# A guard at the start of a kernel becomes part of a decision at its end

## The chip, the cores and the metric

The kernel runs on one core of a Trainium2 chip. The metric is the time of one execution on the device, in microseconds (us); the median of several runs is given. The profile is a record of one execution by the hardware profiler. Its engines are PE (TensorE, matmuls), PEld (its weight loads), DVE (VectorE), ACT (ScalarE), POOL (GpSimd) and SP (SyncE, which here only issues DMAs). A name with q, such as SPq, is that engine's queue of DMA issues, branches and semaphore instructions.

## The reference, cut to what matters

Two layers are applied to 16 graphs of 1024 nodes with 256 features each. Layer 0 is a masked self-attention with a gelu MLP, layer 1 a graph attention; each has a residual.

```python
# layer 0
h = relu(layernorm(x))
qkv = layer_norm(h, gamma1, beta1)            # 8 heads of 32, the same for q, k and v
scores = einsum('bhqd,bhkd->bhqk', qkv, qkv) / sqrt(32)
attn = softmax(where(adj > 0, scores, -inf))
h = h + attn @ qkv
x = x + h + gelu(layer_norm(h, gamma2, beta2) @ W1 + b1) @ W2 + b2
# layer 1
f = relu(layernorm(x));  g = f @ W
logits = (g @ a_1).T + g @ a_2 + (g @ a_12) @ g.T
p = softmax(where(adj > 0, leaky_relu(logits, 0.2), -9e15))
x = x + elu(f @ W_1 + (p @ f) @ W_2)
```

## The kernel before

There are two programs for the same function. `fast_path` leaves out the running maxima of the softmaxes; that is exact enough only while the scores stay small. `general_path` computes them. The top function, `tile_gnn_kernel`, chooses.

Before the fast path it loads gamma1 and beta1 (1 KB each) into one partition (L1525), takes the largest absolute value of each on DVE (L1529), forms 16 max|gamma| + sqrt(32) max|beta| (L1533, L1534) and compares it with a constant (L1535). The result, `bounded`, is read into a register of all five engines (L1539), and each of them branches (L1540). `redo`, one minus that flag, is written at L1538. If the bound holds, `fast_path` runs. It ends with a second test: sums of squares of three weight products and a count of softmax denominators in a good interval were gathered in `seen` along the way; a matmul adds them over the partitions (L1489), four small DVE instructions turn them into `redo` (L1491 to L1496), all engines read `redo` (L1542) and branch (L1543): normally over the general path, to the end.

The fast path handles one graph ("batch", b) after another, with the work of neighbouring batches interleaved. Within it, generators ("streams") issue the instructions: `stream_a` the layer-0 attention, one step per key tile of 128, 32 steps a batch; `stream_b` the rest of layer 0 and all of layer 1 for the batch before; others load, normalize and convert masks. Each stream yields a *place*, a number in batches (1.28 is 28% into the second batch's attention); a loop (L1477 to L1482) always resumes the stream with the lowest place. So places fix the order of instructions on each engine; at the end of `fast_path` a loop (L1498 to L1507) chains all instructions of the current block to that order, engine by engine. `clock` is the planner's own estimate of elapsed time; it decides when deferred pieces are due.

The lines that matter below:

- `prologue` for batch 0: SP loads x (L770) and the mask (L831); DVE takes statistics (L725, L726), ACT rectifies (L787), DVE and POOL make the value tiles (L734, L800, L801), PE transposes them (L808).
- `g1` and `be1`, gamma1 and beta1 broadcast to 128 partitions, are loaded on ACT's queue (L636).
- In the steady part PE makes scores (L975), DVE adds the mask (L996), ACT takes the exponential (L999), PE weighs the values (L1012), and POOL's queue sums the weights by accumulating DMAs (L1036); PE's matmuls of the other layers go through the helper at L570, `po` (L1185) among them.
- `stream_s` (L1469): setup of weight products, then `check_products` from place 1.28 on, one piece per 0.04: `sq`, the square of `wm` (L710), its sum (L712), and the two small products with their sum (L714 to L716). All are DVE instructions.

Of the kernel before, what the change touches and what calls it, by code (L numbers as in the profile page):

```python
# [9 lines left out]
F32 = mybir.dt.float32  # L10
BF16 = mybir.dt.bfloat16
FP8 = mybir.dt.float8e5
I32 = mybir.dt.int32
AF = mybir.ActivationFunctionType
ALU = mybir.AluOpType
# [10 lines left out]
DEN_MIN = 1.0e-24  # L26
DEN_MAX = 1.0e36
ALPHA = 0.2


@with_exitstack
def general_path(
# [125 lines left out]
    with tc.For_i(0, B, 1) as bi:  # L158
# [262 lines left out]
        def logits(t):  # L421
            lp = sc_tile(f"lg_{b}_{t}")
            for dc in range(DC):
# [16 lines left out]

            nc.vector.scalar_tensor_tensor(e, e, ALPHA, e, op0=ALU.mult, op1=ALU.max)
            nc.vector.scalar_tensor_tensor(
                m1[:, 1:2], m1[:, 0:1], ALPHA, m1[:, 0:1], op0=ALU.mult, op1=ALU.max
            )
# [49 lines left out]
def fast_path(  # L494
# [28 lines left out]
    nc = tc.nc  # L523
    B, N, D = x.shape
# [15 lines left out]
    pool = lambda name, bufs, **kw: ctx.enter_context(tc.tile_pool(name=name, bufs=bufs, **kw))  # L540
    const = pool("const", 1)
# [11 lines left out]
    smallp = pool("smallp", 3)  # L553
# [62 lines left out]
    def broadcast_row(src, name):  # L616
        t = const.tile([P, D], F32, name=name)
        rows_to_load.append((t, bass.AP(tensor=src.tensor, offset=src.offset, ap=[[0, P], [1, D]])))
        return t
# [13 lines left out]
    g1 = broadcast_row(gamma1, "g1")  # L633
    be1 = broadcast_row(beta1, "be1")
# [28 lines left out]
    def setup():  # L663
        wl, wa, wT, wb = (lp1.tile([P, DC, D], F32, tag="e1", name=f"stage_{i}") for i in range(4))
        weights_to_load[:0] = [(wl, W), (wa, a_12)]
        for t, src in rows_to_load:
            nc.sync.dma_start(t, src)
        for t, src in weights_to_load:
            nc.sync.dma_start(t, src.rearrange("(c p) n -> p c n", p=P))
        yield  # L670

        for oc in range(DC):
            pt = ps_tile([P, DC, P], f"p_wT_{oc}")
            for ic in range(DC):
                nc.tensor.transpose(pt[:, ic, :], wl[:, ic, oc * P : (oc + 1) * P], ident)
            nc.scalar.copy(wT[:, oc, :], pt.rearrange("p c q -> p (c q)"))
        clock[0] += 0.5
        yield

        def product(dst, lhs, rhs, n, name):  # L680

            for oc in range(DC):
                pp = ps_tile([P, n], f"p_{name}_{oc}")
                for kc in range(DC):
                    matmul(
                        pp,
                        lhs[:, kc, oc * P : (oc + 1) * P],
                        rhs[:, kc, :n],
                        start=(kc == 0),
                        stop=(kc == DC - 1),  # L690
                    )
                nc.scalar.copy(dst[:, oc, :], pp)

        product(wb, wa, wT, D, "wb")
        clock[0] += 1.7
        yield
        product(wm, wT, wb, D, "wm")
        product(w_a2.unsqueeze(2), wT, a2c.unsqueeze(2), 1, "w_a2")
        product(wo2[:, :, D : D + 1], wT, a1c.unsqueeze(2), 1, "w_a1")
        nc.gpsimd.memset(wo2[:, :, D + 1 : D + 2], 0.0)  # L700
        clock[0] += 2.0
        yield

    def check_products():


        sq = lp1.tile([P, DC * D], F32, tag="e1", name="sq")
        few = smallp.tile([P, 2 * DC], F32, tag="few", bufs=1, name="few")
        wmf = wm.rearrange("p c n -> p (c n)")
        nc.vector.tensor_tensor(sq, wmf, wmf, op=ALU.mult)  # L710
        yield
        nc.vector.tensor_reduce(seen[:, 0:1], sq, axis=mybir.AxisListType.X, op=ALU.add)  # L712
        yield
        nc.vector.tensor_tensor(few[:, :DC], w_a2, w_a2, op=ALU.mult)  # L714
        nc.vector.tensor_tensor(few[:, DC:], wo2[:, :, D], wo2[:, :, D], op=ALU.mult)
        nc.vector.tensor_reduce(seen[:, 1:2], few, axis=mybir.AxisListType.X, op=ALU.add)  # L716
        yield
# [25 lines left out]
    def defer(us, f):  # L743
        deferred.append((clock[0] + us, len(deferred), f))

        return clock[0] + us
# [352 lines left out]
    def rest(b, st, tails):  # L1099
# [151 lines left out]
        def weights(c, i):  # L1251
# [18 lines left out]

            nc.vector.scalar_tensor_tensor(e, e, ALPHA, e, op0=ALU.mult, op1=ALU.max)  # L1271
            ready = defer(2.5, lambda: nc.scalar.activation(e, e, AF.Exp, bias=shift))  # L1272
# [196 lines left out]
    def stream_s():  # L1469
        yield -0.3  # L1470
        for i, _ in enumerate(setup()):
            yield 0.25 + 0.05 * i
        yield 1.28
        for i, _ in enumerate(check_products()):
            yield 1.32 + 0.04 * i

    streams = [stream_s(), stream_a(), stream_b(), stream_p(), stream_c(), stream_m()]  # L1477
    places = [next(s, None) for s in streams]
    while any(p is not None for p in places):
        i = min((p, i) for i, p in enumerate(places) if p is not None)[1]  # L1480
# [9 lines left out]
    fit = smallp.tile([1, 2], F32, tag="fit", name="fit")  # L1490
# [2 lines left out]
    nc.vector.scalar_tensor_tensor(  # L1493
        fit[:, 0:1], fit[:, 1:2], float(P * B * NT), fit[:, 0:1], op0=ALU.is_ge, op1=ALU.mult
    )
    nc.vector.tensor_scalar(redo, fit[:, 0:1], -1.0, 1.0, op0=ALU.mult, op1=ALU.add)  # L1496

    last = {}  # L1498
    for i in nc.cur_bb.bb.instructions:
# [10 lines left out]

BOUND = 72.0


def kernel(tc, x, adj, gamma1, beta1, *rest):
    nc = tc.nc
    D = x.shape[2]
    with tc.tile_pool(name="flags", bufs=1) as flags:
        flag = flags.tile([1, 1], I32, name="bounded")  # L1520
        redo = flags.tile([1, 1], I32, name="redo")
        with tc.tile_pool(name="bound", bufs=1) as pool:
            r = pool.tile([1, 2, D], F32, name="bound_rows")
            for i, src in enumerate((gamma1, beta1)):
                nc.sync.dma_start(  # L1525
                    r[:, i, :], bass.AP(tensor=src.tensor, offset=src.offset, ap=[[0, 1], [1, D]])
                )
            m = pool.tile([1, 2], F32, name="bound_max")
            nc.vector.tensor_reduce(  # L1529
                m, r, axis=mybir.AxisListType.X, op=ALU.max, apply_absolute_value=True  # L1530
            )
            s = pool.tile([1, 1], F32, name="bound_sum")
            nc.vector.tensor_scalar_mul(s, m[:, 1:2], math.sqrt(32.0))  # L1533
            nc.vector.scalar_tensor_tensor(s, m[:, 0:1], 16.0, s, op0=ALU.mult, op1=ALU.add)  # L1534
            nc.vector.tensor_scalar(  # L1535
                flag, s, math.sqrt(BOUND * math.sqrt(32.0)), None, op0=ALU.is_le
            )
        nc.vector.tensor_scalar(redo, flag, -1.0, 1.0, op0=ALU.mult, op1=ALU.add)  # L1538
        bounded = nc.values_load(flag[0:1, 0:1], min_val=0, max_val=1)  # L1539
        with tc.If(bounded > 0):  # L1540
            fast_path(tc, x, adj, gamma1, beta1, *rest, redo)
        again = nc.values_load(redo[0:1, 0:1], min_val=0, max_val=1)  # L1542
        with tc.If(again > 0):  # L1543
            general_path(tc, x, adj, gamma1, beta1, *rest)
# [28 lines left out]
```

## Time and profile before

| what | us |
|---|---|
| median of 3 runs | 3482.66 |
| lowest, highest | 3480.26, 3485.44 |
| profiled execution: span, first to last instruction | 3468.1 |
| median less that span: what lies around it | 14.5 |
| PE busy in the span | 3420.8 |
| DVE, ACT, POOL busy | 2746.2, 1858.1, 1419.9 |
| first DMA issue of the branch's rows | 0.76 |
| first load of x | 4.35 |
| first scores on PE (their mask part) | 24.33 |
| last DVE instruction, `redo` | 3462.26 |

The profiled execution is known by its span; the 14.5 us are the difference to the median of the runs. Times in the timeline count from the first instruction. An idle time in brackets is followed by an arrow to what ended it. The accumulating DMAs hold 71.4% of the time of the 16 DMA engines.

### The profile page before, as it was taken

To read this page: it belongs to the slowest core of one execution; us is meant where nothing else is said; L and a number is where in the kernel's file an instruction comes from. 1 tells how busy PE (TensorE), PEld (TensorE's weight loads), DVE (VectorE), ACT (ScalarE), POOL (GpSimd) and SP (SyncE) were. 2 spreads that over 40 slices of the span, in tenths; PEclk is the share of its full clock that TensorE was granted. 3 is DMA by queue.
4 is the path that set the end of the run, shared out by engine and by line. 5 is a ranking of instruction groups with operands and counts; after the bars stand their busy time and mean duration, and the time that the engine had idled before them with its cause. 6 is when DMAs were issued, how large, how long until landed. Compare 5 with 4: busy or idle time off the path is not lost. (4 is left out here: it accounts for less than half of the span.)

```text
span 3468.1 us, 119040 instructions
## 1 busy us (share of the span) xinstructions
PE 3420.8 (99%) x52478; PEld 1650.4 (48%) x52478; DVE 2746.2 (79%) x5194; ACT 1858.1 (54%) x2184; POOL 1419.9 (41%) x1708
## 2 busy tenths in 40 slices
PE   6899999999999999999999999999999999999998
PEld 2244444444444444444444444444444444444477
DVE  6788788787887978878887887878878778887754
ACT  5555555555555555555555555555555555555522
POOL 4444443434434344443444434344344443434220
PEclk9999999999999999999999999999999999999999
DMA  8798989899899998989999899998999989899730
GB/s 194 147 187 172 185 162 192 180 188 191 163 187 175 189 190 165 186 169 190 193 166 189 166 189 185 180 188 168 190 177 194 188 162 184 171 193 185 147 64 14
DMA packets 281906, 598.56 MB, mean 173 GB/s; under 512 B 94882, under 2 KB 130084, under 8 KB 281380
## 3 DMA queue, kind: packets, MB, share of 16 engines
q0 software_dynamic: 124416, 453.04, 71.4%
q1 hardware_dynamic: 156676, 137.56, 15.5%
q8 instruction: 414, 6.78, 0.8%
q14 instruction: 112, 0.92, 0.1%
q10 hardware_dynamic: 288, 0.26, 0.0%
HBM read 104.21 MB, written 16.78 MB: 35 GB/s over the span
## 5 line engine op out<-in xcount | busy, mean ns | idle before, releaser
L999 ACT ACTIVATE e<-e 128x1024 f32<-128x1024 f32 x852 | 895.9, 1057 | 945.9 <-DVE e L996 704.4
L1036 POOL DMA_DIRECT2D acc<-e x864 | 759.6, 896 | 1443.4 <-DMA acc<-e 636.5
L996 DVE TENSOR_TENSOR e<-s,mk 128x1024 f32<-128x1024 f32 x852 | 1004.0, 1218 | 188.3 <-PE s L975 149.4
L975 PE MATMUL s<-kT 32*64 32x512 f32 x8192 | 579.2, 615 | 2.9 <-DVE odd L996 2.2
L1012 PE MATMUL o<-e,va 128*32 128x512 f32 x3456 | 462.3, 605 | 2.1 <-ACT e L999 2.1
L570 PE MATMUL pa<-gw,e 128*32 128x258 f32 x7648 | 453.8, 380 | 0.0
L570 PE MATMUL lg<-fT,uT 128*32 128x256 f32 x7680 | 448.6, 379 | 0.0
L570 PE MATMUL ph<-yT,w 128*32 128x256 f32 x7808 | 447.7, 379 | 0.0
L570 PE MATMUL po<-w,hid 128*32 128x256 f32 x7680 | 439.7, 379 | 0.0
L570 PEld LDWEIGHTS ph<-yT,w 128*32 128x32 f32 x7808 | 259.9, 110 | 197.5 <-issue 42.1
L570 PEld LDWEIGHTS po<-w,hid 128*32 128x32 f32 x7680 | 250.9, 110 | 208.4 <-issue 61.7
L570 PEld LDWEIGHTS lg<-fT,uT 128*32 128x32 f32 x7680 | 258.9, 110 | 189.7 <-issue 38.7
L570 PEld LDWEIGHTS pa<-gw,e 128*32 128x32 f32 x7648 | 251.6, 110 | 199.5 <-issue 48.3
L1272 ACT ACTIVATE e<-e,shift 128x512 f32<-128x512 f32 x256 | 183.2, 717 | 187.1 <-DVE e L1271 159.8
L1266 DVE SCALAR_TENSOR_TENSOR e<-lg,gw,mk 128x256 f32<-128x256 f32 x512 | 223.2, 477 | 71.6 <-PE lg L570 61.1
L1169 DVE TENSOR_TENSOR hid<-ph,b1c 128x512 f32<-128x512 f32 x256 | 175.4, 688 | 86.3 <-PE ph L570 74.8
L1012 PEld LDWEIGHTS o<-e,va 128*32 128x32 f32 x3456 | 69.0, 108 | 353.3 <-issue 221.5
L1271 DVE SCALAR_TENSOR_TENSOR e<-e 128x512 f32<-128x512 f32 x256 | 195.4, 763 | 8.8
L999 ACT ACTIVATE acc<-acc 128x1024 f32<-128x1024 f32 x124 | 131.0, 1057 | 130.4 <-DVE acc L996 125.9
L975 PEld LDWEIGHTS s<-kT 32*64 32x64 f32 x8192 | 121.2, 130 | 163.0 <-issue 106.2
L996 DVE TENSOR_TENSOR acc<-s,mk 128x1024 f32<-128x1024 f32 x124 | 146.1, 1218 | 20.9 <-PE s L975 18.4
L800 POOL TENSOR_TENSOR nrm<-nrm,g 128x256 f32<-128x256 f32 x128 | 114.0, 891 | 61.4 <-DVE nrm L734 61.4
(146 smaller groups left out, 3815.6 us busy)
## 6 DMA issues: line engine op xcount, KB each, us to landing
acc<-e POOLq DMA_DIRECT2D x864, 512.0 KB, 6.1
adj<-in_adj_dram SPq DMA_DIRECT2D x248, 256.0 KB, 5.3
h<-in_x_dram SPq DMA_DIRECT2D x64, 256.0 KB, 5.9
xb<-in_x_dram SPq DMA_DIRECT2D x128, 128.0 KB, 5.1
out_dram<-z SPq DMA_DIRECT2D x128, 128.0 KB, 3.7
adj<-in_adj_dram SPq DMA_DIRECT2D x4, 512.0 KB, 6.6
mk<-mq SPq DMA_TRANSPOSE x128, 6.4
w<-in_L_gnn_W_dram SPq DMA_DIRECT2D x2, 1024.0 KB
```

The source lines that it names most:

```text
L570: nc.tensor.matmul(out[c : c + HD], lhsT[:, c : c + HD], rhs, start=start, stop=stop)
L800: nc.gpsimd.tensor_mul(nrm, nrm, g1)
L975: nc.tensor.matmul(sc[j // 2][c : c + P // 2, j % 2, :], kT[r, g, kt * P + c : kt * P + c + P // 2], kT[r, g, qs], start=j >= by_pe, stop= ...
L996: nc.vector.tensor_tensor(e, masked, mb, op=ALU.add)
L999: weights = lambda e=e, masked=masked: nc.scalar.activation(e, masked, AF.Exp, scale=SCALE)
L1012: nc.tensor.matmul(o[j * HD : (j + 1) * HD, :], va[:, kt, (g * GH + j) * HD : (g * GH + j + 1) * HD], es[j // 2][:, j % 2, :], start=(kt = ...
L1036: nc.gpsimd.dma_start(sums[g, qh][i], e, accum_op=ALU.add)
L1169: nc.vector.tensor_tensor(hid[:, f0 : f0 + 2, :], ph, b1c[:, f0 : f0 + 2].unsqueeze(2).to_broadcast([P, 2, CW]), op=ALU.add,)
L1266: nc.vector.scalar_tensor_tensor(e[:, j, :], lg[:, j, :], gw[:, kt, D : D + 1], st[c // 2][:, kt // 2, qs, kt % 2], op0=ALU.add, op1=ALU.add,)
L1271: nc.vector.scalar_tensor_tensor(e, e, ALPHA, e, op0=ALU.mult, op1=ALU.max)
L1272: ready = defer(2.5, lambda: nc.scalar.activation(e, e, AF.Exp, bias=shift))
```

## The change

The top function now calls `fast_path` at once, with no loads, no flag, no register and no branch ahead of it. The bound is worked out inside `check_products`, as a new first piece, from one partition of `g1` and `be1`, which are in SBUF anyway. The result, `not_bounded`, is 0 or -1 in a constant tile; the last DVE instruction takes it as a factor: redo = fit x not_bounded + 1, where the factor was the constant -1. The pieces of `check_products` are now four, 0.03 of a batch apart, where there were three, 0.04 apart; `sq` moves to 1.32, its sum to 1.35, the small products to 1.38. If the bound does not hold, the fast path has run for nothing and the general path follows; before, the fast path was skipped.

```diff
+    not_bounded = const.tile([1, 1], F32, name="not_bounded")
+
     def check_products():
 
+        m = smallp.tile([1, 2], F32, tag="bound", bufs=1, name="bound_max")
+        for i, r in enumerate((g1, be1)):
+            nc.vector.tensor_reduce(
+                m[:, i : i + 1], r[0:1], axis=mybir.AxisListType.X, op=ALU.max, apply_absolute_value=True
+            )
+        s = smallp.tile([1, 1], F32, tag="bound_sum", bufs=1, name="bound_sum")
+        nc.vector.tensor_scalar_mul(s, m[:, 1:2], math.sqrt(32.0))
+        nc.vector.scalar_tensor_tensor(s, m[:, 0:1], 16.0, s, op0=ALU.mult, op1=ALU.add)
+        nc.vector.tensor_scalar(
+            not_bounded, s, math.sqrt(BOUND * math.sqrt(32.0)), -1.0, op0=ALU.is_le, op1=ALU.mult
+        )
+        yield
 
         sq = lp1.tile([P, DC * D], F32, tag="e1", name="sq")
...
         for i, _ in enumerate(check_products()):
-            yield 1.32 + 0.04 * i
+            yield 1.32 + 0.03 * i
...
-    nc.vector.tensor_scalar(redo, fit[:, 0:1], -1.0, 1.0, op0=ALU.mult, op1=ALU.add)
+    nc.vector.tensor_scalar(redo, fit[:, 0:1], not_bounded, 1.0, op0=ALU.mult, op1=ALU.add)
...
     with tc.tile_pool(name="flags", bufs=1) as flags:
-        flag = flags.tile([1, 1], I32, name="bounded")
         redo = flags.tile([1, 1], I32, name="redo")
-        with tc.tile_pool(name="bound", bufs=1) as pool:
-            r = pool.tile([1, 2, D], F32, name="bound_rows")
-            for i, src in enumerate((gamma1, beta1)):
-                nc.sync.dma_start(
-                    r[:, i, :], bass.AP(tensor=src.tensor, offset=src.offset, ap=[[0, 1], [1, D]])
-                )
-            m = pool.tile([1, 2], F32, name="bound_max")
-            nc.vector.tensor_reduce(
-                m, r, axis=mybir.AxisListType.X, op=ALU.max, apply_absolute_value=True
-            )
-            s = pool.tile([1, 1], F32, name="bound_sum")
-            nc.vector.tensor_scalar_mul(s, m[:, 1:2], math.sqrt(32.0))
-            nc.vector.scalar_tensor_tensor(s, m[:, 0:1], 16.0, s, op0=ALU.mult, op1=ALU.add)
-            nc.vector.tensor_scalar(
-                flag, s, math.sqrt(BOUND * math.sqrt(32.0)), None, op0=ALU.is_le
-            )
-        nc.vector.tensor_scalar(redo, flag, -1.0, 1.0, op0=ALU.mult, op1=ALU.add)
-        bounded = nc.values_load(flag[0:1, 0:1], min_val=0, max_val=1)
-        with tc.If(bounded > 0):
-            fast_path(tc, x, adj, gamma1, beta1, *rest, redo)
+        fast_path(tc, x, adj, gamma1, beta1, *rest, redo)
         again = nc.values_load(redo[0:1, 0:1], min_val=0, max_val=1)
```

More of the change, by code (lines that the diff above doesn't have):

```diff
@@ L28 @@
 ALPHA = 0.2
+BOUND = 72.0
 @with_exitstack
@@ L1507, in fast_path @@
         last[i.engine] = i.name
-BOUND = 72.0
 def kernel(tc, x, adj, gamma1, beta1, *rest):
```

## The prediction

> **What bounds the kernel now.** I read the page's first two parts, then a table of stages (busy time of each engine per stretch), then the timeline of the first 30 us and of 198 to 234 us, where the new work lands, and last the records of the two branch lines.
>
> ```profile
> span 3468.1 us, 119040 instructions
> ...
> PE 3420.8 (99%) x52478; PEld 1650.4 (48%) x52478; DVE 2746.2 (79%) x5194; ACT 1858.1 (54%) x2184; POOL 1419.9 (41%) x1708
> ```
>
> TensorE (PE) is busy for 99% of the span: all but 47 us. The page's slices show where those are, at the two ends above all, and the table of stages says it in numbers (columns: stretch, its length, busy time of PE, PEld, DVE, ACT, POOL with instruction counts, granted clock, DMA share, GB/s):
>
> ```profile
> 0.00:4.35 4.35, 0.00 (x0) 0.00 (x0) 1.25 (x5) 0.00 (x0) 0.21 (x4) 1.00 0.00 0
> 4.35:24.30 19.95, 2.65 (x8) 1.37 (x8) 13.18 (x43) 4.26 (x7) 11.46 (x21) 1.00 0.71 203
> ...
> 31.60:200.00 168.40, 155.07 (x2032) 53.97 (x2024) 129.60 (x205) 99.54 (x112) 75.33 (x90) 0.98 0.81 168
> 200.00:3380.00 3180.00, 3177.97 (x50046) 1528.05 (x50039) 2555.70 (x4823) 1723.63 (x2015) 1330.73 (x1591) 1.00 0.91 177
> ```
>
> In the first 4.35 us PE does nothing and no input of the real work is under way. From 200 to 3380 us PE waits 2.0 us of 3180. What happens in the first 4.35 us is in the timeline (start, duration, engine, line, operation):
>
> ```profile
> 0.76 0.35 SPq L1525 DMA_DIRECT2D bound_rows<-in_L_gnn_gamma_dram  x1
> 1.16 0.22 SPq L1525 DMA_DIRECT2D bound_rows<-in_L_gnn_beta_dram  x1
> 2.49 0.67 DVE L1529 TENSOR_REDUCE bound_max<-bound_rows 1x2 f32<-1x512 f32 x1 [2.49 <-DMA bound_rows<-in_L_gnn_beta_dram]
> ...
> 3.73 0.14 DVE L1538 TENSOR_SCALAR redo<-bounded 1x1 int32<-1x1 int32 x1
> 4.35 0.36 SPq L770 DMA_DIRECT2D h<-in_x_dram  x1
> 4.47 1.28 ACT L611 ACT_TABLE_LOAD   x1 [4.47 <-DVE redo L1538]
> ```
>
> Everything the kernel needs starts behind this chain: SP's first load of x at 4.35, ACT's table load at 4.47, POOL's identity at 4.49.
>
> **The change part by part.** *The start, removed.* SP's first DMA issue is at 0.76. With the two 1 KB loads, the five DVE instructions (2.49 to 3.87), the register load (465 ns on SP) and the compare-and-branch (44 ns) gone, that first issue is the load of x, and it moves from 4.35 to 0.76: **-3.59 us**. Does all else move by as much? ACT and POOL wait for nothing else, so theirs move by about 3.8 to 4.0 and get slack. The next chain begins with x's landing: DVE's first statistics at 7.05, rectify 11.50, value 15.89, transpose 18.66, first scores at 24.33. Each was released by the one before it, back to SP's loads; gamma's and beta's broadcast (ACT queue, 7.04 and 9.36) wait for the landings of the first two SP loads, by their semaphores, and move along. So the whole front moves by 3.59, and since PE has no slack after 200 us, the end does too.
>
> *The five instructions, moved and re-shaped.* They come back at place 1.28 of the schedule, where `sq` (L710) stands now, on DVE at 205.84. One 1x512 reduce took 0.674; it becomes two of 1x256. The rows around are 0.285 for 126 columns (L1097) and 0.679 for 512 (L712), a slope of 1.02 ns per column, so I take 0.42 each. The three small ones took 0.50 from 3.20 to 3.70. Sum 1.38 us of DVE. `sq` (0.68) moves one step on, to where its reduce was (0.68), the reduce goes one further, the three small ones (0.43) last. So DVE gains 0.70 net at 205.8, nothing at 217.3, at most 0.68 near 221 and 0.43 near 227. No DMA is added: the rows g1 and be1 are in SBUF since the start.
>
> What is behind them in DVE's queue, and who waits:
>
> ```profile
> 205.84 0.68 DVE L710 TENSOR_TENSOR sq<-wm 128x512 f32<-128x512 f32 x1
> ...
> 207.28 5.36 PE L570 MATMUL po<-w,hid 128*32 128x256 f32 x96
> ...
> 207.35 2.34 DVE L996 TENSOR_TENSOR e<-s,mk 128x1024 f32<-128x1024 f32 x2
> ...
> 208.59 2.19 ACT L999 ACTIVATE e<-e 128x1024 f32<-128x1024 f32 x2 [0.19 <-DVE e L996]
> ```
>
> The masked scores end at 209.69 and the exponentials at 210.78. PE's next scores (which overwrite the banks) load at 212.57 and its weighted sums at 213.62, both behind its own 5.36 us of `po`; so 2.84 us of cover lie there. Near 221 it is the same: exponentials end at 223.58, wanted at 226.35, 2.77 us. I take the cost as **0**. Without cover it is 1.38; below zero nothing can come of it, since an instruction is added. The shorter steps of the schedule (0.03 for 0.04) change nothing else: the planner's clock is not advanced there.
>
> *The end.* The last DVE instruction gets a pointer where it had a constant: same row, 0.14. SP's 0.18 us of register work and its assert (28 ns) after the first branch go, but the engines that finish last are others: PE's jump over the general path takes 3668 ns, and DVE goes on 3.85 us after its own. That jump stays. I take **0**. From both sides: 0.3 better if DVE's landing came as early as ACT's (3466.01 for 3467.06; then PE's at 3466.77 decides), or 3.85 worse if the shifted code made DVE wait for one more piece.
>
> ```profile
> L1543 PEldq COMPARE_BRANCH  x1: 3668/3668/3668, 3463.0 to 3463.0; - x1
> ```
>
> *The first transfer.* Today two small loads go ahead of x's. If a first transfer is slower, x's pays it now. The first row took 351 ns to issue, the second 223 ns, and they landed 1.27 and 1.22 us after issue. So the nearest row says 0.13 to 0.18; the far end is the slowest load of the first 10 us (7.3 us to landing for 2.7): 4.6. I take 0 and keep the ends.
>
> **Sum.** -3.59 + 0 + 0 + 0: the span goes from 3468.14 to 3464.55. Around it lie 14.52 us (median 3482.66 minus this span), taken as unchanged; the profiled execution has only its span, so I set it level with the median, inside runs that spread from 3480.26 to 3485.44. Forecast **3479.1 us**, 0.10% less. About 0.2%, 7 us, is what a measurement of this kernel can tell from no change.
>
> **The clock, a term with its own dice.** The trace's clock record goes to full at 31.62, to half at 89.65 for 3.41 us, and at 127.19 for 3.41 again: steps of 3.413 us. In the stretches of that length just before, PE was busy 20% and 32%; stretches with 52% and more kept the clock. Cold, 16 score matmuls take 2.00 for 1.11 and 8 weighted sums 1.82 for 1.07, so a dip costs 0.89 + 0.75 = 1.64.
>
> ```profile
> 89.00:94.00 5.00, 4.99 (x48) 1.23 (x55) 4.33 (x9) 2.99 (x3) 0.98 (x2) 0.66 0.92 171
> ```
>
> With the 3.413 us grid moved over PE's gaps in steps of 0.34 us, I count one or two stretches under 45%; I allow one dip less (-1.6) or one more (+1.6). The warm-up can stay where it is while PE starts earlier: 3.59 x 0.85 busy x 0.45 lost = 1.4 worse; or come a step earlier: 3.41 x 0.85 x 0.45 = 1.3 better. [...]
>
> **The rivals.**
> - *The clock takes some of it back, or adds to it.* Unlucky: 1.4 for the warm-up and one dip more, 1.6: 3482.1. Lucky: 1.3 and one dip less, 1.6: 3476.2, near the edge of what can be told. For it: PE waits 13 us between 31.6 and 200, and two dips are there. Against a large effect: the count stays at one or two. Chances 0.15 and 0.13.
> - *DVE becomes the wait (slower than before).* If the group at 205.8 delays the masked scores by more than PE's 2.84 us of cover, ACT and the accumulating DMAs behind it slip a turn; ACT's longest wait for that DVE line is 6.8 us, giving 3479.1 + 6.8 = 3485.9. It decides from 2.84 us; against it stand 0.70 net and 1.38 at most. For it: DVE is busy 4.91 of 5 us there. Chance 0.08.
> - *It doesn't do what it says:* the 3.59 come back in front of x's landing (a slow first transfer, 4.6 at most): 3482.7 to 3483.7. Chance 0.06.
> - *Forecast:* 3479.1, by itself 3476.5 to 3481.7 from the spread of the runs. Chance 0.58.
>
> **How the numbers follow.** The range, 3475.0 to 3485.0, takes in both clock cases, the ends of the first transfer and of the last jump; it leaves out most of the DVE case (0.07), the outer third of the lucky clock (0.04) and 0.05 for the spread of runs. Faster by over 0.2% (under 3475.7): the lucky clock with a spread to the same side, 0.08, and the forecast's own spread, 0.04; together 0.12. Slower by over 0.2% (over 3489.6): the DVE case with a second turn lost, 0.05. The rest, 0.83, lies within.
>
> **What would show it.** Right: SP's first issue is the load of x near 0.76, first scores near 20.7, `sq` near 213.7 (one step on, 217.3, less 3.6), PE still 5.00 of 5 us from 200 to 236, the jump at the end as long as before, span near 3464.6. Wrong: x lands later than 2.7 us after issue; a PE wait on DVE appears near 202 to 228; the clock record shows another number of dips; or DVE's landing after the last branch moves by more than 0.3. A difference of over 7 us would mean that something outside the first 30 us and the last 6 has changed, which nothing here foresees.

## The result and the profile after

The changed kernel took 3471.33 us in the median of 22 runs (3463.87 to 3477.07), the kernel before 3476.52 in 22 runs beside them (3466.91 to 3487.01): ratio **0.9979, 95% interval 0.997 to 0.9988**, 5.2 us less. The forecast was 3479.1 with a range from 3475.0; the time lies below the range. Of the 7.8 us between forecast and result, 6.1 are the level from which it was counted (3482.66 for 3476.52) and 1.6 the size of the gain (3.6 for 5.2).

The page's head and the table of stages of the changed kernel (the second stage runs from the first issue of x to 20.70, as long as the one shown of before):

```profile
span 3463.8 us, 119015 instructions
...
PE 3421.5 (99%) x52478; PEld 1644.7 (47%) x52478; DVE 2751.4 (79%) x5194; ACT 1857.5 (54%) x2184; POOL 1416.9 (41%) x1708
```

```profile
0.00:0.76 0.76, 0.00 (x0) 0.00 (x0) 0.00 (x0) 0.01 (x1) 0.22 (x5) 1.00 0.00 0
0.76:20.70 19.94, 1.85 (x5) 0.87 (x6) 13.03 (x42) 4.25 (x7) 10.64 (x20) 1.00 0.73 202
...
28.01:200.00 171.99, 161.59 (x2116) 56.41 (x2108) 134.01 (x216) 103.13 (x116) 77.25 (x92) 0.97 0.81 171
200.00:3380.00 3180.00, 3177.20 (x49982) 1523.17 (x49981) 2559.98 (x4825) 1720.60 (x2014) 1326.90 (x1590) 1.00 0.91 177
```

PE is busy for as long as before (3421.5 for 3420.8), so the gain is idle time of PE. In these two executions 2.8 us of it are gone ahead of 50 us and 2.9 between there and 185 us; from 200 to 3380 us PE waits 2.8 us, for 2.0 before. The start of the timeline:

```profile
0.75 1.28 ACT L612 ACT_TABLE_LOAD   x1 [0.75 <-PEq L1553]
0.76 0.40 SPq L785 DMA_DIRECT2D h<-in_x_dram  x1
...
1.68 0.42 SPq L785 DMA_DIRECT2D h<-in_x_dram  x1
...
3.46 0.43 DVE L740 BATCH_NORM_STATS2 st_a<-h 128x6 f32<-128x256 f32 x1 [1.81 <-DMA h<-in_x_dram]
...
7.24 0.43 DVE L740 BATCH_NORM_STATS2 st_a<-h 128x6 f32<-128x256 f32 x1 [2.40 <-DMA h<-in_x_dram]
```

x's first load is issued at 0.76 instead of 4.35, and its statistics start 2.70 us behind the issue, as before. The new work near 200 us:

```profile
200.59 0.40 DVE L711 TENSOR_REDUCE bound_max<-g 1x1 f32<-1x256 f32 x1
...
200.92 0.40 DVE L711 TENSOR_REDUCE bound_max<-be 1x1 f32<-1x256 f32 x1
...
201.35 0.14 DVE L715 TENSOR_SCALAR bound_sum<-bound_max 1x1 f32<-1x1 f32 x1
201.46 0.73 POOL L1127 TENSOR_TENSOR h<-h,b2r 128x256 f32<-128x256 f32 x1
201.53 0.67 DVE L716 SCALAR_TENSOR_TENSOR bound_sum<-bound_max,bound_sum 1x1 f32<-1x1 f32 x1
...
202.23 0.14 DVE L717 TENSOR_SCALAR not_bounded<-bound_sum 1x1 f32<-1x1 f32 x1
```

Five instructions, 1.75 us of DVE, while PE was busy for 36.00 of the 36 us from 200 to 236:

```profile
200.00:236.00 36.00, 36.00 (x586) 17.31 (x588) 32.62 (x78) 21.40 (x22) 17.08 (x20) 1.00 1.03 214
```

And the last branch:

```profile
L1535 PEldq COMPARE_BRANCH  x1: 3395/3395/3395, 3458.9 to 3458.9; - x1
```

The last DVE instruction takes 200 ns with its pointer, for 142 before; from its start to the end of the span there are 5.82 us, for 5.88.

### The profile page after: what moved, and what is told of

Its sections match the earlier page's. It is cut to its first block, busy times and chain, and to the rows that moved or that the text cites. A ratio compares the mean times of both kernels' runs of the same rounds, so it can differ in the third digit from the quotient of the medians.

```text
span 3463.8 us, 119015 instructions
## 1 busy us (share of the span) xinstructions
PE 3421.5 (99%) x52478; PEld 1644.7 (47%) x52478; DVE 2751.4 (79%) x5194; ACT 1857.5 (54%) x2184; POOL 1416.9 (41%) x1708
```

## Theories and experiments

Three accounts of why it is 5 us rather than 3.6 follow. **A**: the front's 3.6 come out one for one, and the rest is chance of the executions. **B**: the new places of the DVE pieces give the rest. **C**: an earlier start is worth more than its length, because waits on the accumulating DMAs go with it.

"Front" below is read at a copy on ACT near 50 us, behind all of the start: 52.22 in the profiled execution of before, 49.42 in that of the changed kernel. Means of runs are compared where medians of few runs would be coarse; intervals that are given for differences in us come from resampling the runs.

**The halves and a dose, on the full kernel.** The start alone: the changed kernel without the bound, whose result is taken as true, and with the old places.

```diff
-        m = smallp.tile([1, 2], F32, tag="bound", bufs=1, name="bound_max")
...
-            yield 1.32 + 0.03 * i
+            yield 1.32 + 0.04 * i
...
-    nc.vector.tensor_scalar(redo, fit[:, 0:1], not_bounded, 1.0, op0=ALU.mult, op1=ALU.add)
+    nc.vector.tensor_scalar(redo, fit[:, 0:1], -1.0, 1.0, op0=ALU.mult, op1=ALU.add)
```

> The change with only its first half: no loads, no flag and no branch at the start; the bound is worked out nowhere (so that test is left out), and the three check pieces stand where they stood before, 0.04 apart. Theory A (the start alone: what the front gains comes out at the end one for one, and everything beyond is spread between executions): first scores on PE at 21.5 us, 2.8 earlier than before's 24.3, as in the changed kernel, and the time 2.8 to 3.6 us under before, ratio 0.9990 to 0.9992. Theory B (the new place of the DVE pieces gives the rest of the gain): the front as in A, ratio about 0.9990, and the changed kernel's 0.9979 only together with the move. Theory C (an earlier start also avoids waits in the first batch, on the accumulating DMAs above all, so it is worth more than it is long): ratio 0.998, 6 to 7 us.

The move alone: the kernel before, with the bound worked out a second time in check_products and the new places.

> The other half: loads, flag and branch at the start stay, and the bound is worked out a second time in the second batch, with the pieces 0.03 apart, as in the changed kernel; redo takes both. Theory A: front and time as before, ratio 1.000 within 0.1%; in the trace PE busy 5.0 of 5 us at each stretch from 200 to 240 us. Theory B: 2 to 4 us faster, ratio 0.9990. Theory C: 1.000.

The dose (the same delay, made longer): the kernel before, with its first reduce done 15 times.

```diff
-            nc.vector.tensor_reduce(
-                m, r, axis=mybir.AxisListType.X, op=ALU.max, apply_absolute_value=True
-            )
+            for _ in range(15):
+                nc.vector.tensor_reduce(
+                    m, r, axis=mybir.AxisListType.X, op=ALU.max, apply_absolute_value=True
+                )
```

> The kernel before with the first reduce at the start done 15 times instead of once, nothing else: 14 x 0.71 = 9.9 us more ahead of the branch (a dose of the same delay). Theory A: first scores at 34.2 us and the time 9.9 us longer, ratio 1.0028. Theory C (a start's shift is worth about twice its length): 18 to 20 us longer, ratio 1.0055. A rival in which the front is hidden behind something that does not move: ratio 1.000.

And the kernel before unchanged, as a measure of chance.

> The kernel before once more, unchanged: what the comparison itself can tell. All theories: ratio 1.000, the interval shows the noise; Theory A in particular needs single executions of one and the same program to differ by 10 us or more (before: 3466.9 to 3487.0) with the same start, the differences coming in steps at waits on the accumulating DMAs and at half-clock stretches.

Against the kernel before (median 3479.16): start alone 3474.76, ratio 0.9991 (0.9978 to 1.0003); move alone 3476.03, 0.999 (0.9976 to 1.0004); long chain 3485.03, 1.002 (1.0007 to 1.0033); unchanged 3475.92, 0.9987 (0.9971 to 1.0003). The unchanged kernel "gains" as much as the halves: nothing below 4 us is told apart here. Inconclusive, but for the dose: its interval, 2.4 to 11.5 us, takes in the 9.9 of A and leaves out the 18 to 20 of C.

**Where the spread comes from.** Behind 200 us the distance between two profiled executions of the full kernel changes in steps of up to some 5 us, also where the kernel is the same. PE's waits on the accumulating DMAs there differ from execution to execution (0 to 2.2 us in total), so these DMAs were the suspects, and the next base has none. It is called quiet below: each normaliser is taken from one partial sum, scaled, instead of from the accumulated one. Its results are not the reference's. Three constants (`SHIFT`, `DEN_MIN`, `DEN_MAX`) are widened to suit and POOL sets one more constant tile; every other instruction stays.

```diff
-            if b == 0 and kt % 2:
+            if True:
...
-        nc.scalar.copy(ds, den)
+        nc.scalar.activation(ds, den, AF.Identity, bias=many, scale=8.0)
```

> The kernel before without its accumulating DMAs (L1036): the weights of layer 0 are no longer summed over the key tiles, so the softmax denominators of layer 0 come from a part of them (scaled by 8, plus 300), and the shift of layer 1's exponentials and the limits of its denominators are widened to suit. All other instructions stay. It asks where the spread between executions comes from. If from waits on those DMAs: single executions then lie within some 5 us instead of 20 (standard deviation under 2 us, for about 6 with them), the time some 5 to 10 us lower, ratio 0.997 to 0.999. If the spread comes from elsewhere (the clock, loads, code), the standard deviation stays at 4 to 6 us.

> The changed kernel with the same work left out as in the run before it. Against that run, with little noise left, Theory A (the front's gain comes out one for one, 2.8 to 3.6 us, and the measured 0.21% holds spread or an offset of the comparison besides) gives 2.5 to 4.0 us less. Theory C (an early start is worth twice its length because waits on the accumulating DMAs are avoided) cannot act here and gives the same 2.8 to 3.6; so the full kernels' difference, if it stays at 6 to 7 us with these DMAs, would speak for C.

On the same chip also both full kernels again:

> The changed kernel once more, in one call with an unchanged kernel (the next run). Theory A: 2.8 to 3.6 us less than that unchanged one, whatever the ratio to the shared runs of before (if the comparison has an offset, both show it: the unchanged kernel 0.9987 once before, so 0.998 here). Theory C: 6 to 7 us less than the unchanged one.

> The kernel before, unchanged, a second time. If the 0.9987 of the first time was chance, the ratio is 1.000 here; if the comparison gives any second kernel an offset, it is again 0.998 to 0.999, and the effect of a change has to be read against this run and not against 1.

Quiet before 3461.8 (3460.79 to 3465.01), quiet changed 3456.63 (3455.02 to 3458.54); changed again 3472.32, ratio 0.9988 (0.9976 to 1.0001); unchanged again 3479.15, 1.001 (0.9999 to 1.002). Without the accumulating DMAs the kernels are 16 to 17 us faster, and their runs lie within some 4 us (5 and 6 runs, standard deviations 1.3 and 1.5) where those of the full kernels beside them lie within 14 to 18 (12 to 23 runs, standard deviations 4.1 to 6.0): most of the spread comes with these DMAs. The gain stays: so C, in the form that it needs those DMAs, does not carry the larger part.

**The halves and the dose on the quiet base.** The same edits on that base, one chip:

> The kernel before without its accumulating DMAs once more (denominators taken from one partial sum, so the normalisation is not the reference's), as the base of this call. All theories: 3461.8 within 1 us, as the first time, with a spread of under 5 us between lowest and highest.

> The change's first half alone on the quiet base: the bound is worked out nowhere (its result is taken as true), check_products keeps its old places, no accumulating DMAs. If the earlier start comes out one for one (A), 3.3 to 3.7 us below the quiet kernel before; if the new place of the DVE pieces gives the rest (B), also 3.3 to 3.7 below, and the quiet changed kernel 1.5 to 2 below this one; if an earlier start is worth more than its length even without the accumulating DMAs (C), 5 to 5.7 below.

> The second half alone on the quiet base: the start with loads, chain and branch is kept, and the bound is worked out a second time in check_products, with the new places. A and C: within 0.7 us of the quiet kernel before. B: 1.5 to 2 us below it.

> The kernel before on the quiet base with its first reduce done 15 times, which puts the front 9.9 to 10.3 us later. One for one (A): 9.5 to 10.7 us above the quiet kernel before. If the front counts for more than its length (C): 14 to 16 above. If less (waits further on take some of it up): under 9.

Medians: before 3460.53, start alone 3456.88, move alone 3462.19, long chain 3470.56. Against both measurements of the quiet kernel before taken together (15 runs, mean 3461.5):

| quiet kernel | front moved by, us | time moved by, us (95%) |
|---|---|---|
| start alone | -3.8 | -4.3 (-5.8 to -2.9) |
| changed (both measurements) | -3.7 | -4.6 (-5.8 to -3.3) |
| move alone | -0.1 | 0.0 (-1.2 to +1.0) |
| long chain | +9.6 | +9.5 (+8.4 to +10.6) |

B falls on this base: the move alone gives nothing, and the start alone gives what the whole change gives. The dose comes out one for one, as A has it. (On the full kernel the halves were too small to be told from chance.) What the dose is, the timeline of the long chain shows: 15 reduces, and x's load right behind the chain.

```profile
2.50 10.59 DVE L1532 TENSOR_REDUCE bound_max<-bound_rows 1x2 f32<-1x512 f32 x15 [2.50 <-DMA bound_rows<-in_L_gnn_beta_dram]
...
14.28 0.37 SPq L772 DMA_DIRECT2D h<-in_x_dram  x1
```

**The rest on the quiet base is for the most part the clock.** From the front to an ACT instruction near 180 us (`hid`), and from there to the end, in the profiled executions:

| quiet kernel | front to `hid`, us | half-clock time in it, us | `hid` to end, us |
|---|---|---|---|
| start alone | 125.16 | 0 | 3278.83 |
| changed | 126.35 | 3.4 | 3279.13 |
| before | 128.76 | 6.8 | 3278.70 |
| move alone | 129.66 | 6.8 | 3278.67 |
| long chain | 129.65 | 6.8 | 3278.49 |
| changed, second | 130.22 | 10.2 | 3278.59 |
| before, second | 130.41 | 10.2 | 3278.87 |
| chain without branch (below) | 128.49 | 10.2 | 3279.03 |
| x first (below) | 129.21 | 10.2 | 3278.93 |

Behind 180 us all agree within 0.64 us. Ahead of it they differ by up to 5.25, for the most part with the time that PE spent at half clock, and not by kernel: the changed kernel has 126.35 in one execution and 130.22 in another. The table of stages, from the front to `hid`, for start alone and for the second before (the clock is the 1.00 and the 0.96 behind POOL's column):

```profile
48.80:173.96 125.16, 115.72 (x1588) 41.29 (x1572) 103.83 (x176) 77.49 (x91) 36.84 (x42) 1.00 0.23 61
```

```profile
52.68:183.09 130.41, 120.84 (x1588) 42.22 (x1572) 104.97 (x176) 77.59 (x92) 35.59 (x42) 0.96 0.23 58
```

The same 1588 matmuls are busy 5.12 us longer: nearly the whole 5.25. Against the execution without any, one half-clock stretch of 3.41 us comes with 1.19 us, two with 3.60 to 4.50, three with 3.33 to 5.25: 1.1 to 2.25 a stretch, so not all of a difference is the clock's.

**What in the start it was, and one more step.** The changed kernel on the quiet base once more, measured beside the runs that follow:

> The changed kernel without its accumulating DMAs once more (normalisation not the reference's), as the base of this call. One for one with the front (A): 3457.5 within 1 us (the quiet kernel before at 3461.2, less 3.7). If more than the front comes out (C): 3456.6 or less again.

The rows and the chain put back ahead of x, without register load and branch; the chain's last instruction writes the buffer that x's load overwrites:

```diff
+            for i, src in enumerate((gamma1, beta1)):
+                nc.sync.dma_start(
+                    r[:, i * D : (i + 1) * D], bass.AP(tensor=src.tensor, offset=src.offset, ap=[[0, 1], [1, D]])
+                )
...
+            nc.vector.tensor_scalar(
+                h[0][0:1, 0, 0:1], s0, math.sqrt(BOUND * math.sqrt(32.0)), None, op0=ALU.is_le
+            )
```

> The changed kernel on the quiet base with the two row loads and the four DVE instructions put back ahead of x's first load, whose buffer the last of them writes, so that the load waits for them; no register load and no branch. If the place of x's load is what counts: its issue at 3.9 to 4.3, 3.2 to 3.6 later than in the quiet changed kernel, and the time 3.0 to 3.7 us above that kernel's. If the register load and the branch themselves held everything up: within 1 us of the quiet changed kernel.

Both x loads first:

```diff
-            for f, i in ((load, 0), (fetch, 0), (load, 1), (fetch, 1), (fetch, 2), (fetch, 3), (load, 2), (load, 3)):
+            for f, i in ((load, 0), (load, 1), (fetch, 0), (fetch, 1), (fetch, 2), (fetch, 3), (load, 2), (load, 3)):
```

> The changed kernel on the quiet base, with the second x load issued ahead of the first adj load. Its issue comes 0.46 earlier, and its landing, now 5.56 us behind its issue with a 512 KB adj load ahead of it, should come 1.5 to 2 us earlier; the statistics of the second x tile from 7.24 to some 5.5. One for one (A): 1 to 2 us below the quiet changed kernel. If the front is then held by the first adj load and its mask instead: within 0.7 us of it.

> The same order of loads in the full changed kernel, with its accumulating DMAs. One for one (A): 5 to 6 us below the kernel before (3.7 for the start and 1 to 2 for the order), 0.9982 to 0.9986; if the order gains nothing, as the changed kernel, 0.998 to 0.999.

Quiet changed kernel 3457.69; with the chain and no branch 3461.14, in the mean 3.4 above both measurements of the quiet changed kernel (1.5 to 5.0). Its timeline:

```profile
2.47 0.67 DVE L862 TENSOR_REDUCE max<-rows 1x2 f32<-1x512 f32 x1 [0.82 <-DMA rows<-in_L_gnn_beta_dram]
...
3.54 0.14 DVE L868 TENSOR_SCALAR h<-sum 1x1 f32<-1x1 f32 x1
3.71 0.36 SPq L787 DMA_DIRECT2D h<-in_x_dram  x1
```

x's load waits for the landing of the rows and the four DVE instructions, and that alone brings most of the time back; ACT and POOL start at 0.74 here and it does not help. With register load and branch x was issued at 4.34 to 4.58: their part is 0.6 to 0.9 of the 3.6.

Both x loads first, quiet: 3456.78; the mean is 0.9 below the quiet changed kernel (-2.6 to +0.8), which decides nothing. The trace says why it is little:

```profile
4.97 0.42 DVE L742 BATCH_NORM_STATS2 st_a<-h 128x6 f32<-128x256 f32 x1
...
7.47 0.69 DVE L851 TENSOR_SCALAR mq<-adj 128x1024 fp8e5<-128x1024 int32 x1 [1.07 <-DMA adj<-in_adj_dram]
```

The second x tile's statistics start at 4.97 instead of 6.59 to 6.76, but DVE then waits 1.07 us for the first adj, and 1.1 to 1.3 of the step are left at the front: both accounts of that expectation hold in part. In the full kernel: 3470.79, ratio 0.9977 (0.9959 to 0.9994). For the last open point both full kernels ran again:

> The changed kernel a third time. One for one with the front (A): ratio 0.999 within 0.0013, what the two repeats of the unchanged kernel strayed by. If 6 to 7 us are real (C): 0.9981 within the same.

> The changed kernel with both x loads first, a second time. One for one with the front: 1.1 to 1.6 us below the changed kernel of this call, which a spread of 5 us hides; a first result of 8.5 us below before in the median would then shrink to 4.5 to 5.5. If the first result holds, 8 to 9 again.

Changed 3472.94, ratio 0.998 (0.9965 to 0.9996); x first 3469.14, 0.9973 (0.9962 to 0.9984). Over both comparisons x first is 2.0 us below the three of the changed kernel in the mean (-4.4 to +0.4): the fastest version here, but its lead over the changed kernel is not shown.

**The excess on the full kernel.** The means of all full comparisons, one number for each group of runs:

| kernel | means, us | front, profiled executions, us |
|---|---|---|
| before (with its unchanged repeats) | 3477.5, 3480.2, 3478.0, 3480.9, 3480.0, 3480.6, 3476.3, 3480.4 | 52.22, 53.12, 53.39 |
| changed | 3470.8, 3474.2, 3474.1 | 49.42, 49.05, 49.30 |
| start alone | 3474.7 | 48.88 |
| move alone | 3475.9 | 52.78 |
| x first | 3471.1, 3470.0 | 47.86, 48.15 |
| long chain | 3485.8 | 62.48 |

Eight groups of before average 3479.2, three of the changed kernel 3473.0: 6.2 less. Groups of one kernel stray by some 1.7 us (their standard deviation), so the 6.2 carry about 2.7 either way (t interval, 9 degrees of freedom), and 3.7 lies just inside. Counted by its front, the move alone belongs to before and the start alone to the changed kernel; with both the difference is 5.4, 2.5 either way. Between the changed kernel and the long chain the front differs by 13.2 and the time by 12.8: one for one over that distance, which speaks against C, where both steps would be worth more than their length. Whether before itself really lies 2.5 us above that line **stays open**.

## Why the prediction was wrong, point by point

- **The step that failed** is the level from which the gain was taken off: "Around it lie 14.52 us (median 3482.66 minus this span), taken as unchanged; the profiled execution has only its span, so I set it level with the median". Around the span lie 1.76 us (3465.53 of its own time for 3463.77); in all but one of the profiled executions that followed it was 1.8 to 1.9, in that one 3.3. So the profiled execution of before took about 3469.9, near the lower end of a kernel whose runs went from 3466.91 to 3487.01, and the three runs shown were from the upper half. The base was set by three runs of a kernel that strays by 20 us, and the range with it. From the median of 22 runs, 3476.5, the same gain gives 3472.9, and a range as wide around it holds the measured 3471.33.
- **The start, -3.59**: right. x is issued at 0.76 as forecast. The first scores came at 21.53, not near 20.7: 2.80 earlier, since in before's profiled execution the second x tile had its statistics at 10.03, in six others with the same start at 10.25 to 11.26, and with the changed start at 6.59 to 7.24, the last of these in the profiled execution of the changed kernel. Front to front, over three executions each, the shift is 3.65.
- **The first transfer, 0**: right, 2.70 us from issue to statistics in both.
- **The five instructions, 1.38 us of DVE at a cost of 0**: the cost is right, the size was short by 0.37. The reduces took 0.40 each for the 0.42 taken; the fourth took 0.67 for 0.15. PE kept 36.00 of 36 us there, and the move alone on the quiet base gave 0.0 (-1.2 to +1.0), so the DVE rival, 3485.9, did not come about. `sq` stood at 212.08, 1.6 earlier than forecast, because the whole batch was earlier by then.
- **The end, 0**: right; 58 ns more in the last instruction, 5.82 us to the end for 5.88.
- **The span**: 3464.55 forecast, 3463.8 measured. That agreement is partly luck: one execution on each side, and the shift went from 2.80 at 70 us to 5.25 near 185 us, 6.29 near 700, 3.98 near 1500 and 4.4 at the end. On the way lay half-clock stretches (two in before, three in the changed kernel) and waits such as these two (the table of waits, before and then changed; total, times, longest), which other executions of the same kernels have in other sizes.

```profile
PE den L914 <- DMA acc<-e: 2.5, 1, 2.5
```

```profile
PE den L929 <- DMA acc<-e: 1.4, 1, 1.4
```

- **The clock**: right as dice, 1.64 a stretch forecast and 1.1 to 2.25 measured; the number of stretches (one to two, one more or less) was none to three, five in one full execution. The warm-up's price was wrong: the full clock came at 28.3 to 31.6 us in three executions of before and at 28.5 to 29.6 in three of the changed kernel, so hardly earlier, and yet the front kept its 3.65; the 1.4 set down for that were not paid. Nor does an early full clock show as a gain at the front: in the start alone it came at 24.02, 4.5 us or more ahead of the three of the changed kernel, and the front stood at 48.88 for 49.05 to 49.42. The full clock came 15.6 to 20.1 us behind the first normalisation in the three executions of before (31.62 for 11.50 in the first of them), so it kept no fixed distance from it; what sets its time was not shown.
- **The chances**: 0.12 stood on faster by over 0.2%; the ratio says 0.21% with an interval from 0.12% to 0.30%, on the border itself. The range was too narrow on the low side, by the failed step.

## What to carry to other kernels

Before a median is used as a base, look at how far the runs of the kernel stray, and put the profiled execution in that spread by its own time, not by the difference to the median. Where a change is smaller than the spread, take out what makes the spread (here the accumulating DMAs, by another operand) and measure the halves and a dose there. In this kernel, in which PE is busy from end to end (99% of the span), what stood ahead of the first load of the real work cost its length once (on the quiet base from 3.8 us less to 9.6 us more): a check that can wait belongs behind it.

## What the runs showed of the hardware

- A DVE instruction on one element took 0.67 us: `bound_sum` (L716) reads two tiles and ended at 202.20, as did POOL's 128x256 addition that had begun 0.07 us ahead of it (201.46 and 0.73). In the move alone on the quiet base the same pair ended at 203.10 and 203.09. At the start of before, with POOL idle, the same instruction took 148 ns. `nm` (L797), the same operation on two tiles of 128x2, takes 95 to 161 ns in 63 of its 64 executions, but 0.45 us in this one, where it ends 0.02 us behind POOL's addition (one of 0.44 to 0.46 us stands in each of the traces here):

```profile
94.98 0.73 POOL L816 TENSOR_TENSOR va<-nrm,be 128x256 f32<-128x256 f32 x1
95.28 0.45 DVE L797 SCALAR_TENSOR_TENSOR nm<-mv_a,rs_a 128x2 f32<-128x2 f32 x1
```

  By these ends the long ones finished with POOL's instruction. Not every overlap does this: at 21.34 `nm` took 161 ns inside POOL's power on 128x2 (L745), which had begun 0.07 us ahead of it and ended 0.46 us behind it. No run moved `bound_sum` away from POOL's addition, so that POOL held it up is inferred from the ends and not shown.
- The accumulating DMAs cost 16 to 20 us of some 3479 (medians 17.1 and 15.7 us apart in one comparison, 19.9 in another), and most of the spread between runs: standard deviations of 3.0 to 7.9 us with them, 1.3 to 2.2 without.
- PE's jump over the general path took 3395, 3672 and 3792 ns in three executions of the changed kernel, and 3363 to 3908 over all kernels here: this branch has a spread of its own.
